# The last norm's factors multiplied in behind the product with W, and sent there over DRAM

## The chip, the cores and the metric

The kernel runs on one core of one Trainium2 chip. The metric is the device time of one launch in microseconds (us); lower is better. Unless a single run is named, times are medians of the fast runs of a kernel, with the lowest and highest in brackets. The engines are TensorE (PE; PEld is its weight load), VectorE (DVE), ScalarE (ACT), GpSimd (POOL) and SyncE (SP), which issues nearly all transfers of this kernel, in order.

## The reference, cut to what matters

The input is 4 images of 128 channels and 64 x 64 points, so 16,384 tokens of 128 values. Layer 0 is a convolution with window attention. Layer 1 is a linear attention and a feed-forward part, each behind a normalisation of every token. The change touches the last normalisation and the product with W that follows it.

```python
def _ln_t(v, eps=1e-5):                      # each token on its own
    m = jnp.mean(v, axis=-1, keepdims=True)
    s = jnp.var(v, axis=-1, keepdims=True)
    return (v - m) / jnp.sqrt(s + eps)

def _L1_ffn_ref(x, W, V, gamma, beta):
    Wx = jnp.einsum('bti,hi->bth', x, W)
    # mean and variance of Wx over all tokens, then normalised by them
    # ... then y_t = sigmoid(wx_t + y_{t-1} V^T), a scan over the tokens
...
t = _to_tokens(layer0(x))
t = t + _L1_attn_ref(_ln_t(t), ...)
t = t + _L1_ffn_ref(_ln_t(t), ...)           # the last norm and W
```

The statistics over all tokens mean that nothing of the final part can start before the last token's product with W is there. Hence the kernel has a long middle, band after band, and a tail.

## The kernel before

The tokens are worked off in 16 bands of 1024 (two halves of 512 in layer 1, four windows in layer 0). PE alternates between the window attention of one band and layer 1 of the band before. A half's tokens stand on the partitions (128 tokens by 4 groups); its last norm writes `xn`, four transposes on PE turn it, ACT copies it out of the bank, and the product with W follows. Besides that, the residual stream `h.x` is turned as well (`keep`), since it is needed at the end.

```python
ENGINES = [... for e in ("PE", "DVE", "Activation", "Pool")]    # held to the source's order; SP is not
...
    def keep(h):
        rs = p1.tile([P, SEG, HSEGS], F32, tag="rs_o", name="rs_o")
        nc.scalar.copy(rs, turned(h.x, 0, 4).rearrange("p (k s) -> p s k", s=SEG))
        nc.sync.dma_start(resd[h.b][:, h.hb], rs.rearrange("p s k -> p (s k)"))

    def turn_last(h):                        # four transposes and a copy
        h.xl = p2.tile([P, 512], F32, tag="xl2", name="xl2")
        nc.scalar.copy(h.xl, turned(h.xn, 0, 4))

    def product(h):
        wps = bank()
        nc.tensor.matmul(wps, fwT, h.xl, start=True, stop=True)
        nc.scalar.copy(wx[:, h.b, h.hb], wps.rearrange("p (k s) -> p s k", s=SEG))
        nc.vector.bn_stats(stats[:, h.b * NH + h.hb, :], ...)
```

The window attention has a small round trip of its own: the softmax's denominators are packed into `dc`, inverted, written to DRAM (`rd`) and read back spread over the partitions (`rden`); GpSimd multiplies the heads' output by it (`oT`), and the output projection on PE needs `oT`.

```python
        nc.sync.dma_start(dc, den[::HD, :])
        ...
        nc.vector.reciprocal(rc, dc)
        rd = dram4.tile([HEADS, BR * WT], F32, tag="rd", name="rd")
        nc.sync.dma_start(rd.rearrange("h (a e) -> (h a) e", e=16), rc)
        rden = p1.tile([P, BR * WT], F32, tag="rden", name="rden")
        nc.sync.dma_start(rden, rd.unsqueeze(1).to_broadcast([HEADS, HD, BR * WT]))
```

## Time and profile before

| | before |
|---|---|
| time | 935.57 us (933.84 to 939.02), 3 runs |
| mean granted clock of PE | 0.975 |
| PE, DVE, ACT, POOL busy | 94%, 80%, 58%, 28% |
| one band in the middle | 50.3 us |
| transfers | 53,045 packets, 63.46 MB |

PE is the bound: from 100 to 800 us it has work in 99 to 100% of the time at full clock, and the other engines have slack. The lines for this stand in the prediction.

```profile
DVE dc L423 <- DMA dc<-den: 7.5, 4, 3.4
```

A line number below, such as L221, is the line in the kernel that is being shown; the change and the experiments move lines by a few.

### The profile page before, as it was taken

The numbers are of one execution on the slowest core, as the hardware profiler recorded it, in microseconds if no ns is written. First come the engines' busy times: TensorE is split into PE (matmuls) and PEld (weight loads), VectorE is DVE, ScalarE is ACT, GpSimd is POOL, SyncE is SP. The second block draws the span as 40 slices with busy tenths as digits, with TensorE's granted clock in tenths as the row PEclk, the third lists the DMA queues.
The fourth block names the chain that finished last, engine by engine and source line by source line (L and its number), as shares of the span: only waits on it lengthen the run. The fifth ranks groups of instructions, "written<-read, shape, count | busy, mean of one in ns | idle before, by whom it ended". The sixth has DMA issues, their size and how long they took to land.

```text
span 930.9 us, 26534 instructions
## 1 busy us (share of the span) xinstructions
PE 876.9 (94%) x10508; PEld 656.1 (70%) x10508; DVE 741.1 (80%) x2452; ACT 539.1 (58%) x1010; POOL 262.4 (28%) x359
## 2 busy tenths in 40 slices
PE   4978999999999999999999999999999999987985
PEld 3756777877777777777787777787777777755442
DVE  6464978888897988797988888798878786676886
ACT  3755566565756565656656575656566665422552
POOL 2122131413232322313041323232232312121184
PEclk9988999999999999999999999999999999988897
DMA  4111121121222121212121121212121111102853
GB/s 121 34 44 56 47 72 37 54 57 57 59 63 59 49 57 50 69 49 73 37 56 57 52 59 60 62 48 62 48 66 48 49 37 60 43 24 73 345 205 129
DMA packets 53045, 63.46 MB, mean 68 GB/s; under 512 B 22960, under 2 KB 33840, under 8 KB 52400
## 3 DMA queue, kind: packets, MB, share of 16 engines
q1 hardware_dynamic: 51184, 56.91, 19.8%
q10 hardware_dynamic: 1728, 4.77, 1.3%
q8 instruction: 85, 1.39, 0.6%
q14 instruction: 48, 0.39, 0.1%
HBM read 35.44 MB, written 17.30 MB: 57 GB/s over the span
## 4 chain that ended last, share of the span: by engine, by line
PE 60%; DVE 26%; issue 4%; ACT 4%; DMA 3%; POOL 3%; ACTq 0%; SPq 0%; DVEq 0%; POOLq 0%
DVE y L288 8%; PE bank L337 8%; PE bank L465 6%; PE bank L382 6%; PE bank L212 6%; PE bank L494 5%; PE bank L400 4%; PE bank L350 4%; PE bank L412 4%; PE bank L602 3%; DVE st L191 2%; PE bank L815 2%; PE bank L537 2%; PE bank L573 2%; DVE state L562 2%
## 5 line engine op out<-in xcount | busy, mean ns | idle before, releaser
L288 DVE SCALAR_TENSOR_TENSOR y<-ypad,cpe_w,y 128x512 f32<-128x512 f32 x240 | 189.8, 791 | 15.1 <-ACT y L286 11.7
L391 ACT ACTIVATE es<-bank 128x512 f32<-128x512 f32 x256 | 132.2, 603 | 77.1 <-PE bank L382 77.1
L440 POOL TENSOR_TENSOR oT<-o_sb,rden 128x512 f32<-128x512 f32 x64 | 86.6, 1354 | 243.1 <-DMA rden<-rd 165.8
L195 POOL TENSOR_SCALAR rs<-mv 128x4 f32<-128x4 f32 (+2 forms) x100 | 25.1, 251 | 364.4 <-DVE mv L193 163.2
L203 DVE TENSOR_SCALAR xn<-x,mv,rs 128x128 f32<-128x128 f32 x256 | 90.8, 416 | 26.5 <-POOL rs L196 26.5
L196 POOL TENSOR_TENSOR rs<-rs,mhalf 128x4 f32<-128x4 f32 (+2 forms) x100 | 106.2, 1062 | 8.3
L382 PEld LDWEIGHTS bank<-q,k 32*128 32x128 f32 x3072 | 97.7, 189 | 7.8 <-ACT k L345 6.6
L382 PE MATMUL bank<-q,k 32*128 32x96 f32 (+1 forms) x3072 | 96.3, 270 | 1.1 <-ACT k L345 1.1
L412 PEld LDWEIGHTS bank<-es,v_sb 128*32 128x32 f32 x3072 | 56.8, 110 | 30.2 <-issue 18.6
L465 PE MATMUL bank<-woT,oT 128*128 128x128 f32 x512 | 68.1, 289 | 5.7 <-POOL oT L440 5.7
L465 PEld LDWEIGHTS bank<-woT,oT 128*128 128x128 f32 x512 | 64.8, 202 | 9.7 <-POOL oT L440 7.3
L412 PE MATMUL bank<-es,v_sb 128*32 128x96 f32 (+1 forms) x3072 | 70.1, 240 | 0.0
L494 PE MATMUL bank<-xl,awT 128*128 128x512 f32 x128 | 70.0, 630 | 0.0
L400 PE MATMUL bank<-es,ones 128*32 128x512 f32 x512 | 69.1, 612 | 0.0
L357 ACT COPY v_sb<-bank 128x512 f32<-128x512 f32 x64 | 37.5, 586 | 53.5 <-PE bank L350 42.2
L337 PE MATMUL bank<-y2w,wqT 128*128 128x256 f32 x256 | 66.4, 382 | 1.0 <-DVE y2w L288 1.0
L337 PE MATMUL bank<-y2w,wkT 128*128 128x256 f32 x256 | 65.8, 380 | 0.0
L350 PE MATMUL bank<-wvT,y2w 128*128 128x256 f32 x256 | 65.8, 380 | 0.0
L345 ACT COPY q<-bank 128x512 f32<-128x512 f32 x64 | 37.6, 587 | 41.3 <-PE bank L337 39.2
L345 ACT COPY k<-bank 128x512 f32<-128x512 f32 x64 | 37.3, 583 | 36.8 <-PE bank L337 36.7
L191 DVE BATCH_NORM_STATS2 st<-x 128x6 f32<-128x128 f32 x256 | 55.5, 280 | 1.1
L337 PEld LDWEIGHTS bank<-y2w,wqT 128*128 128x128 f32 x256 | 45.8, 194 | 12.8 <-issue 7.2
(124 smaller groups left out, 1728.4 us busy)
## 6 DMA issues: line engine op xcount, KB each, us to landing
rden<-rd SPq DMA_DIRECT2D x64, 256.0 KB
v_sb<-v_sb SPq DMA_DIRECT2D x128, 64.0 KB
resd<-rs_o SPq DMA_DIRECT2D x32, 256.0 KB
out<-ot SPq DMA_DIRECT2D x32, 256.0 KB
xin<-in_xt SPq DMA_DIRECT2D x15, 512.0 KB
res<-resd SPq DMA_DIRECT2D x2, 2048.0 KB
res<-resd ACTq DMA_DIRECT2D x2, 2048.0 KB
dc<-den SPq DMA_DIRECT2D x64, 8.0 KB
```

Source lines behind the costliest of these rows:

```text
L196: nc.gpsimd.tensor_tensor(rs[:, :n], rs[:, :n], mhalf[:, :n], ALU.pow)
L203: nc.vector.tensor_scalar(xn[:, j, :], piece, mv[:, j, 0:1], rs[:, j : j + 1], ALU.subtract, ALU.mult)
L288: nc.vector.scalar_tensor_tensor(y2, src, cpe_w[:, tap : tap + 1], y2, ALU.mult, ALU.add)
L337: nc.tensor.matmul(pps[:, br * WT : (br + 1) * WT], wT[:, br * P : (br + 1) * P], y2, start=True, stop=True,)
L350: nc.tensor.matmul(vps[:, e * 256 : (e + 1) * 256], y2[:, e * P : (e + 1) * P], wvT, start=True, stop=True,)
L382: nc.tensor.matmul(sps[h][:, cols], w["k"][rows, k0 : k0 + P], w["q"][rows, cols], start=False, stop=(br, n) == pieces[-1],)
L391: nc.scalar.activation(es, sps[h], AF.Exp, scale=scale)
L400: nc.tensor.matmul(dps[rows], ones[:, :HD], w["es", h], start=True, stop=True)
L412: nc.tensor.matmul(ops[rows, cols], w["v"][:, n, c0 : c0 + HD], w["es", h][:, cols], start=(br, n) == pieces[0], stop=(br, n) == pieces[-1],)
L440: nc.gpsimd.tensor_tensor(oTs[n][:, :, :, wj * WS : (wj + 1) * WS], w["o"].rearrange("p (a r c) -> p a r c", a=BR, c=WS), w["rden"].rearra ...
L465: nc.tensor.matmul(yps[:, j * P : (j + 1) * P], oT[:, br, t], woT[:, br, :], start=br == 0, stop=br == BR - 1,)
L494: nc.tensor.matmul(zps, awT[:, m * P : (m + 1) * P], h.xl, start=True, stop=True)
```

## The change

The intent is to take work off PE. A norm is (x - m) r with a mean m and a factor r for each token. If W is centred once (each row minus its mean), then W (x - m) r = (Wc x) r: the product can be applied to the turned residual stream, which `keep` makes anyway, and the factor r multiplied in behind it. The transposes of `xn` and two ACT copies fall away. But behind the product the tokens stand on the free axis, so their factors are needed as a row, the same on all 128 partitions. They go there over DRAM: a small transfer `send` writes 512 factors, and a broadcast `spread` reads them back into `rs_b`. Both are issued ahead of time, and SP is held to the source's order too. The load of the band after next is issued one window later. Two buffer counts change as well and are not in the cut below: `xn` has two buffers instead of three, `rs_o` two instead of one.

```diff
-ENGINES = [getattr(mybir.EngineType, e) for e in ("PE", "DVE", "Activation", "Pool")]
+ENGINES = [getattr(mybir.EngineType, e) for e in ("PE", "DVE", "Activation", "Pool", "SP")]
...
+    def send(h):
+        h.there = dram4.tile([SEG, 4, P // SEG], F32, tag="rs_d", name="rs_d")
+        nc.sync.dma_start(h.there.rearrange("s j n -> n s j"), h.found[2])
+
+    def spread(h):
+        h.rs = p2.tile([P, 512], F32, tag="rs_b", name="rs_b")
+        nc.sync.dma_start(h.rs, h.there.rearrange("s j n -> (s j n)").partition_broadcast(P))
...
-    def turn_last(h):
-        h.xl = p2.tile([P, 512], F32, tag="xl2", name="xl2")
-        nc.scalar.copy(h.xl, turned(h.xn, 0, 4))
...
-        nc.tensor.matmul(wps, fwT, h.xl, start=True, stop=True)
-        nc.scalar.copy(wx[:, h.b, h.hb], wps.rearrange("p (k s) -> p s k", s=SEG))
+        nc.tensor.matmul(wps, fwT, h.xs.rearrange("p s k -> p (s k)"), start=True, stop=True)
+        w = wx[:, h.b, h.hb].rearrange("p s k -> p (s k)")
+        nc.vector.tensor_tensor(w, wps, h.rs, ALU.mult)
...
-            (norm, z), (product, y), None,
+            (send, z), None,
             (output0, a), (measure, a), None,
-            (turn_last, z), None,
+            (product, y), (spread, z), None,
... (the second half of the order and the end likewise)
-        if i < len(places) and wj == 1 and n + 2 < len(bands):
+        if i < len(places) and wj == 2 and n + 2 < len(bands):
             load(n + 2)
```

With `SEG` = 32 the tensor in DRAM is 32 x 4 x 4 values, and each of the 512 factors is a run of 4 bytes of its own. The order is that in which the product's columns stand, so that the multiply reads its factors straight.

More of the change, by code (lines that the diff above doesn't have):

```diff
@@ L80, in conv_attn_hybrid @@
     )
+    center = const.tile([P, P], F32, name="center")
+    nc.vector.tensor_scalar(center, ident, -1.0 / P, None, ALU.add)
     mhalf = const.tile([P, NCH], F32, name="mhalf")
@@ L139, in prepare, with centre @@
         nc.vector.tensor_scalar(ab1, ab[:, :2], 1.0, None, ALU.add)
+    def centre(w):
+        cps = bank()[:, : w.shape[1]]
+        nc.tensor.matmul(cps, center, w, start=True, stop=True)
+        nc.vector.tensor_copy(w, cps)
     dmax = const.tile([P, 16], F32, name="dmax")
@@ L484, in norm @@
     def norm(h):
-        h.xn = normed(h.found, p3, "xn")
+        h.xn = normed(h.found, p2, "xn")
     def turn(h):
@@ L587, in attend @@
             nc.vector.scalar_tensor_tensor(x, nv[:, i, :P], rd[:, i, :], x, ALU.mult, ALU.add)
-    def keep(h):
-        rs = p1.tile([P, SEG, HSEGS], F32, tag="rs_o", name="rs_o")
-        nc.scalar.copy(rs, turned(h.x, 0, 4).rearrange("p (k s) -> p s k", s=SEG))
-        nc.sync.dma_start(resd[h.b][:, h.hb], rs.rearrange("p s k -> p (s k)"))
-    def turn_last(h):
-        h.xl = p2.tile([P, 512], F32, tag="xl2", name="xl2")
-        nc.scalar.copy(h.xl, turned(h.xn, 0, 4))
+    def send(h):
[4 more added lines that the diff above has]
+        nc.sync.dma_start(h.rs, h.there.rearrange("s j n -> (s j n)").partition_broadcast(P))
+    def keep(h):
+        h.xs = p2.tile([P, SEG, HSEGS], F32, tag="rs_o", name="rs_o")
+        nc.scalar.copy(h.xs, turned(h.x, 0, 4).rearrange("p (k s) -> p s k", s=SEG))
+        nc.sync.dma_start(resd[h.b][:, h.hb], h.xs.rearrange("p s k -> p (s k)"))
     def product(h):
         wps = bank()
-        nc.tensor.matmul(wps, fwT, h.xl, start=True, stop=True)
-        nc.scalar.copy(wx[:, h.b, h.hb], wps.rearrange("p (k s) -> p s k", s=SEG))
-        nc.vector.bn_stats(
-            stats[:, h.b * NH + h.hb, :], wx[:, h.b, h.hb].rearrange("p s k -> p (s k)")
-        )
+        nc.tensor.matmul(wps, fwT, h.xs.rearrange("p s k -> p (s k)"), start=True, stop=True)
+        w = wx[:, h.b, h.hb].rearrange("p s k -> p (s k)")
+        nc.vector.tensor_tensor(w, wps, h.rs, ALU.mult)
+        nc.vector.bn_stats(stats[:, h.b * NH + h.hb, :], w)
     def layer1(n, last):
@@ L633, in layer1 @@
             (scores, c), (keep, a), None,
-            (accumulate, c), (norm, a), None,
+            (accumulate, c), (send, a), None,
             (attend, c, 0), None,
-            (turn_last, a), (attend, c, 1), (measure, c), None,
+            (attend, c, 1), (measure, c), (spread, a), None,
         ]
@@ L647, in layer1_end @@
     def layer1_end(y, z):
-        norm(z)
+        send(z)
+        keep(z)
+        yield
         product(y)
-        yield
-        keep(z)
-        turn_last(z)
+        spread(z)
         yield
@@ L709, in conv_attn_hybrid @@
                 behind = layer1(m, halves.pop(m - 1, (None, None)))
+        if i == 2:
+            centre(fwT)
         between(i, 0)
```

## The prediction

> **What bounds the kernel now.** I read the page's busy table first, then the busy time by stretches, then the groups of instructions, and last the timeline of one band of 1024 tokens (the middle of the run repeats every 50.3 us, one band each, 16 bands).
>
> ```profile
> PE 876.9 (94%) x10508; PEld 656.1 (70%) x10508; DVE 741.1 (80%) x2452; ACT 539.1 (58%) x1010; POOL 262.4 (28%) x359
> ...
> 300.00:400.00 100.00, 99.14 (x1282) 76.11 (x1278) 84.66 (x287) 61.57 (x113) 28.98 (x41) 1.00 0.20 56
> 700.00:800.00 100.00, 99.79 (x1320) 76.81 (x1314) 77.56 (x257) 60.70 (x112) 23.48 (x31) 1.00 0.16 48
> 800.00:850.00 50.00, 43.96 (x358) 33.65 (x358) 37.33 (x141) 15.25 (x27) 9.79 (x13) 0.93 0.09 30
> ```
>
> From 100 to 800 us TensorE (PE) is never without work and its clock is 1.00. The second engine, VectorE (DVE), has 15% slack, ScalarE (ACT) 38%. Before 100 and after 800 us the program is bound by latency instead. So in the middle only PE time counts, and at the two ends only the length of chains.
>
> Busy PE time overstates a matmul, because they overlap. I therefore take each group's cost as the distance from its start to the next group's start. Four groups of transposes of the normalised tokens (xn) run in each band:
>
> ```profile
> 471.39 1.01 PE L212 MATMUL bank<-ident,xn 128*128 128x128 f32 x4
> 472.23 0.39 PE L573 MATMUL bank<-v,aT 128*128 128x129 f32 x2
> ...
> 482.15 0.60 PE L212 MATMUL bank<-ident,xn 128*128 128x128 f32 x4
> 482.58 1.03 PE L337 MATMUL bank<-y2w,wkT 128*128 128x256 f32 x4
> ```
>
> These two are the ones that the change removes (first half and second half of a band). The first costs 0.84 us, because it is fed by DVE writing its four pieces just then (1.11 us); the second, whose pieces are long ready, costs 0.43 us. The groups' table would have suggested far more, 4 x 288 ns = 1.15 us each.
>
> ```profile
> L203 DVE TENSOR_SCALAR xn<-x,mv,rs 128x128 f32<-128x128 f32 x256 | 90.8, 416 | 26.5 <-POOL rs L196 26.5
> L212 PE MATMUL bank<-ident,xn 128*128 128x128 f32 x256 | 46.1, 288 | 5.1 <-DVE xn L203 4.8
> L604 DVE BATCH_NORM_STATS2 stats<-wx 128x6 f32<-128x512 f32 x32 | 22.1, 689 | 29.6 <-ACT wx L603 29.5
> L472 DVE TENSOR_TENSOR x<-bank,xin 128x512 f32<-128x512 f32 x32 | 21.9, 685 | 33.7 <-PE bank L465 33.7
> L603 ACT COPY wx<-bank 128x512 f32<-128x512 f32 x32 | 20.1, 629 | 3.9 <-PE bank L602 3.9
> L597 ACT COPY xl<-bank 128x512 f32<-128x512 f32 x32 | 18.8, 588 | 20.7 <-PE bank L212 20.7
> ```
>
> **What the Trainium skill says.** "Perfetto Trace Analysis", section Identifying the Most-Contended Engine, says that matmul occupancy is no good measure for TensorE, as pipelined instructions distort it. The trace agrees: 0.43 us from start to start against 0.60 us of busy time. "DMA: Bandwidth & Descriptors", section Why a DMA increments its semaphore by 16 and not by 1, says that a transfer uses the largest number of engines up to 16 that divides the slowest dimension of both sides. The trace agrees for the existing broadcast rden, whose outer dimension is the 4 heads: its packets fill a share of 0.24 to 0.26, four engines of 16, and it lands 5.3 us after its issue:
>
> ```profile
> 42.27 0.59 SPq L431 DMA_DIRECT2D rden<-rd  x1
> 47.54 1.27 POOL L440 TENSOR_TENSOR oT<-o_sb,rden 128x512 f32<-128x512 f32 x1 [13.54 <-DMA rden<-rd]
> ```
>
> The same page, section Rules for kernel authors, says that a non-contiguous last dimension becomes one descriptor per element; no run here shows that yet, but the new small transfer is of that kind. "TensorE: Matmul & The Clock Gate", section Part 1: The HAM clock gate, says that idleness halves the clock. The trace agrees: after PE idled 4.4 us at 59 us, one round of logits took 2.89 us instead of 1.48. So stalls at the ends cost about double.
>
> **The change, part by part.**
>
> Removed from PE: 32 groups of four transposes. Per band 0.84 + 0.43 = 1.27 us. The product itself stays, and one 128x128 matmul that centres W is added once.
>
> Removed from DVE: the normalisation of 32 halves. In the timeline the two of a band last 1.11 and 2.06 us (the second runs beside a GpSimd multiply). Added: a multiply of a bank by the spread factors, 128x512; by the same shape of L472, 0.69 us each. Net per band 3.17 - 1.38 = 1.8 us less. Removed from ACT: two copies per half, 588 + 629 ns, 2.4 us per band. Neither engine bounds, so this is worth nothing directly.
>
> Added on the queue: per half a send of 512 single values (4 bytes each) and a broadcast of 256 KB. The send's outer dimension is 4, so I expect four engines with 128 descriptors each. The 128 descriptors of dc took 1.1 engine-us altogether (shares 0.12 and 0.22 of 16 engines over 0.2 us each), 9 ns each; at 9 to 12 ns the send needs 1.1 to 1.5 us on its engines. With the 1.5 us that rd needs from issue until rden can follow (804.74 to 806.27), the send should take 2.5 to 3 us (estimate). The broadcast has 128 rows outermost, so 16 engines: 8 packets of 2 KB each at some 110 ns (rden's 32 packets per engine in 3.5 us), about 0.9 us plus latency, 2.5 to 3 us when nothing is ahead of it (estimate).
>
> Moved: the first half's product goes two slots later, behind the output projection L465. So PE reaches L465 sooner, by 1.06 us (the product) and 0.84 us (the transposes). But L465 needs oT, which follows rden: issued at 471.12, oT started at 477.26, ended at 478.53, and PE used it at 479.39. Slack 0.86 us. In the new order I count 5.1 us of PE work from the start of that window's logits to L465, and oT ready at about 5.5 us. So PE will stall there for some 0.4 to 0.5 us, and the saving is 1.27 - 0.45 = 0.8 us per band. Over some 15 bands: -12 us.
>
> The second half's factors are the tight ones on DVE. Its broadcast is issued right behind rden, waits on the four shared engines, and lands some 17.5 us into the window; DVE would want it at 15.7. That is a stall of 1.8 us, but DVE stood there for 1.8 us before too (stats waiting for wx, 29.5 us over 18 waits). I take it as neutral: the transposes that follow find their pieces just in time.
>
> Ends. Start: the load of the third band, which was issued at 11.7 us, now stands in the queue in front of dc at about 44 us, so the early stall grows: +1 us. Between 800 and 850 us two groups of transposes leave a chain that PE latency sets: -2 us. At the very end the last half had normalise, turn, copy, product, copy, statistics: rs at 852.38, statistics at 857.31. Now send, broadcast, multiply: 2.7 + 2.8 + 0.7 = 6.2 us against 4.9, and the reload of the residual stream waits for the multiply as well: +2 us.
>
> Sum: -12 + 1 - 2 + 2 = -11, that is 935.6 - 11 = about 924 us.
>
> **The rivals.**
>
> First, everything hides: no stall at L465, and DVE's freed time removes the rest of PE's small waits (2.5 us on x at L212, some 4 us at L575). Then 1.27 + 0.4 us per band, 25 us in all, ends still +1: about 911. For it speaks that the change was evidently arranged around the waits; against it the 0.86 us slack of oT.
>
> Second, the factors' round trip over DRAM takes the removed work's place: if the 4-byte writes are much slower than I estimate, or the broadcast queues behind rden and the loads, DVE stands 3 us longer per band, the convolution's taps come late, and PE waits for turned tokens by 1 to 2 us. Then the gain is eaten: 935 to 945. For it speaks that DVE and the queue both work strictly in order; against it DVE's 15% slack, and that the change takes another 1.8 us per band from it.
>
> Third, the naive sum: 128 transposes at 288 ns, 37 us, giving 899. The start-to-start distances speak against it.
>
> Fourth, the order of the transfers alone does something: in the middle no PE wait is put down to a DMA, so I expect nothing there.
>
> **Range and chances.** The size per band is the uncertainty: 0.2 to 1.6 us times 15 is -3 to -24, with the ends -2 to +5. So 911 to 936. Faster by over 2% means under 916.9, a gain of 18.7 us, which needs nearly all of the 1.27 us: 0.15. Slower by over 2% would need a new stall of 2.5 us per band beyond the saving: 0.02.
>
> **What would show it.** The distance between bands should fall from 50.3 to about 49.5 us; PE should wait for oT at L465 in most bands; the new multiply on DVE should wait 1 to 2 us for its broadcast in the second halves and not in the first; packets should rise by 32 x 512 + 32 x 128 = 20,480, less a little; the send should take about 2.7 us. Last product to last statistics should be longer by about 2 us. The prediction is wrong if bands fall by 1.5 us or more (then L465 doesn't wait), or if PE waits for DVE after the multiply.

## More of the kernel before

One more view is of use for what follows, the chain of work that ended last, followed back from the last instruction; the shares are of the span:

```profile
PE 60%; DVE 26%; issue 4%; ACT 4%; DMA 3%; POOL 3%; ACTq 0%; SPq 0%; DVEq 0%; POOLq 0%
```

Only 3% of the chain is a transfer. Two waits for the small round trip, of SP's queue and of DVE over the whole span, serve for comparison later (us in total, times, longest):

```profile
SPq L431 <- DMA rd<-rc: 51.4, 45, 2.1
```

## The result, and the profile after

The changed kernel takes 1148.60 us (1145.22 to 1151.02, 4 runs) against 935.64 us (933.84 to 939.02) of the kernel before in the same rounds. The ratio is 1.2268, with a 95% interval of 1.2216 to 1.2320: slower by 23%. A ratio here is always the mean time of one kernel's fast runs over the mean of the other's of the same rounds, so it is not quite the ratio of the medians quoted.

The prediction of 924 us was wrong, in direction and by far more than its range. First the page of the changed kernel: its busy time, then the chain that ended last, by engine and by line.

```profile
PE 926.3 (81%) x10382; PEld 684.2 (60%) x10382; DVE 712.0 (62%) x2358; ACT 510.3 (44%) x946; POOL 257.9 (22%) x359
...
DMA 39%; DVE 27%; PE 23%; issue 4%; POOL 3%; ACT 3%; SPq 1%; ACTq 0%; DVEq 0%; POOLq 0%
DMA rd<-rc 10%; DVE y L297 7%; DMA rs_b<-rs_d 7%; DMA dc<-den 7%; DMA rden<-rd 6%; DMA rs_d<-rs 5%; DVE st L200 3%; PE bank L346 3%; PE bank L474 3%; PE bank L503 2%; PE bank L391 2%; DMA res<-resd 2%; PE bank L221 2%; PE bank L359 2%; PE b
```

The engines did what they were meant to: PE has 126 matmuls fewer (10,508 to 10,382), DVE is busy for 29.1 us less. But transfers now hold 39% of the chain instead of 3%. The striking point is which: the new ones (`rs_d` and `rs_b`) hold 12%, and the old round trip of the softmax denominators (`dc`, `rd`, `rden`) 23%. The busy time by stretches says the same of the middle. Its columns are busy us and instructions of PE, PEld, DVE, ACT and POOL, then the granted clock, the share of the DMA engines, and GB/s:

```profile
300.00:400.00 100.00, 77.69 (x955) 60.60 (x951) 58.22 (x220) 42.83 (x78) 22.67 (x34) 0.91 0.24 50
```

No engine is busy for more than 78% of the time here, and the DMA engines' share is 0.24. So this is a chain of waits. PE's and DVE's waits between 100 and 1000 us, and the waits of SP's queue over the whole span, name the links (us in total, times, longest):

```profile
PE bank L221 <- DVE xn L212: 117.7, 25, 10.5
PE bank L474 <- POOL oT L449: 15.7, 13, 3.7
```

```profile
DVE wx L619 <- DMA rs_b<-rs_d: 105.9, 13, 9.7
DVE dc L432 <- DMA dc<-den: 97.0, 16, 11.6
```

```profile
SPq L440 <- DMA rd<-rc: 154.7, 64, 8.2
...
SPq L606 <- DMA rs_d<-rs: 132.9, 18, 12.1
```

PE waits for DVE's norm; DVE waits for the factors and for `dc`; SP waits up to 12.1 us until a `send` has landed and it may issue the broadcast, and up to 8.2 us for `rd` (2.1 before).

The timeline of one band shows the mechanism; it is a band with two of the longest waits (PE's 25 waits for `xn` last 4.7 us in the mean). First SP's queue (start, length of the issue), without the `v_sb` loads:

```profile
506.30 0.55 SPq L601 DMA_DIRECT2D rs_d<-rs  x1
...
518.27 0.32 SPq L606 DMA_DIRECT2D rs_b<-rs_d  x1
...
519.15 1.89 SPq L414 DMA_DIRECT2D dc<-den  x1
521.09 0.57 SPq L601 DMA_DIRECT2D rs_d<-rs  x1
528.12 0.32 SPq L438 DMA_DIRECT2D rd<-rc  x1
532.19 0.54 SPq L440 DMA_DIRECT2D rden<-rd  x1
```

From the issue of the first `send` until the broadcast may follow are 12.0 us. Everything behind it in the source's order is held up with it: `dc` is issued only at 519.15, although ACT had its source `den` ready at 511.8. The broadcast and the store of the residual stream, 256 KB each, go out just before `dc`, the second `send` right behind it. What DVE and PE do meanwhile (the brackets give the idle time before and what ended it):

```profile
527.62 0.17 DVE L432 TENSOR_TENSOR dc<-dc,pad_c 128x16 f32<-128x16 f32 x1 [11.22 <-DMA dc<-den]
```

```profile
529.92 1.15 PE L221 MATMUL bank<-ident,xn 128*128 128x128 f32 x4 [10.19 <-DVE xn L212]
```

DVE works in order, stands for 11.22 us at `dc`, and so comes late to the norm that PE needs: PE stands for 10.19 us. Then its clock is down, at 0.50, and the round of logits at 531.40 takes 2.72 us where it took 1.48. Of the 11.22 us 2.75 lie before the issue of `dc`, the rest between its issue and its landing; over the whole run it is 33 of 108 us. `rd`, issued at 528.12, takes 4.1 us until `rden` may follow. SP's timeline shows in each of 14 bands one `rd` that is issued while a `send` is on its way: these take 3.5 to 8.6 us, 7.2 in the median, the other 50 of the run 1.5. So the small transfers are not only issued late; those on the way together with a `send` land late too. A stretch of 2 us in this wait, with the same columns as above, shows how idle the transfers themselves are:

```profile
524.00:526.00 2.00, 0.00 (x0) 0.00 (x0) 0.00 (x0) 0.00 (x0) 0.00 (x0) 0.50 0.01 0
```

From 524.0 to 527.6 hardly anything moves: no engine works, 0 GB/s, a DMA share of 0.01 to 0.09. The core waits for writes that the records hardly count as work.

At the end, the queue is quiet, and a `send` is seen with nothing big beside it (the store issued in front of it has moved its last packet at 1048.6):

```profile
1048.36 0.53 SPq L601 DMA_DIRECT2D rs_d<-rs  x1
1057.70 0.31 SPq L606 DMA_DIRECT2D rs_b<-rs_d  x1
```

It takes 9.3 us for 2 KB, and 11.8 the second time (1058.07 to 1069.82), with the store of the residual stream beside it. The prediction had 2.5 to 3. The DMA records tell where in these 9.3 us the time is. In two stretches of it:

```profile
1049.50:1050.40 0.90, 0.64 (x4) 0.28 (x2) 0.83 (x6) 0.00 (x0) 0.00 (x0) 1.00 0.31 2
1054.00:1057.70 3.70, 0.00 (x0) 0.00 (x0) 0.00 (x0) 0.00 (x0) 0.00 (x0) 1.00 0.00 0
```

All 512 packets, of 9 ns each, are recorded in the 0.9 us from 1049.52 to 1050.40. From there until the broadcast may follow, 7.3 us, the DMA share is 0.00. So what is long is not the packets' recorded time but the time from the last packet to the landing.

Where the time came from, along the run: I cut each profiled run at the start of the first output projection of the second band and of the fourteenth. Before: 126.3 us to the first cut, 604.0 for the 12 bands between (50.3 each), 200.6 to the end. After: 126.1, 764.4 (63.7 each), 258.8. So the middle lost 160.4 us, the end 58.2, the start nothing.

### The profile page after: what moved, and what is told of

It reads as the page before. It is cut to its first block, busy times and chain, and to the rows that moved or that the text cites.

```text
span 1149.3 us, 26192 instructions
## 1 busy us (share of the span) xinstructions
PE 926.3 (81%) x10382; PEld 684.2 (60%) x10382; DVE 712.0 (62%) x2358; ACT 510.3 (44%) x946; POOL 257.9 (22%) x359
## 4 chain that ended last, share of the span: by engine, by line
DMA 39%; DVE 27%; PE 23%; issue 4%; POOL 3%; ACT 3%; SPq 1%; ACTq 0%; DVEq 0%; POOLq 0%
DMA rd<-rc 10%; DVE y L297 7%; DMA rs_b<-rs_d 7%; DMA dc<-den 7%; DMA rden<-rd 6%; DMA rs_d<-rs 5%; DVE st L200 3%; PE bank L346 3%; PE bank L474 3%; PE bank L503 2%; PE bank L391 2%; DMA res<-resd 2%; PE bank L221 2%; PE bank L359 2%; PE bank L520 2%
## 5 line engine op out<-in xcount | busy, mean ns | idle before, releaser
L297 DVE SCALAR_TENSOR_TENSOR y<-ypad,cpe_w,y 128x512 f32<-128x512 f32 x240 | 184.9, 771 | 14.3 <-ACT y L295 10.8
L221 PE MATMUL bank<-ident,xn 128*128 128x128 f32 x128 | 34.2, 404 | 130.5 <-DVE xn L212 129.7
L391 PEld LDWEIGHTS bank<-q,k 32*128 32x128 f32 x3072 | 111.7, 212 | 3.9 <-ACT k L354 1.8
L619 DVE TENSOR_TENSOR wx<-bank,rs_b 128x512 f32<-128x512 f32 x32 | 22.0, 689 | 147.3 <-DMA rs_b<-rs_d 140.0
L391 PE MATMUL bank<-q,k 32*128 32x96 f32 (+1 forms) x3072 | 110.2, 295 | 1.1 <-ACT k L354 1.1
L221 PEld LDWEIGHTS bank<-ident,xn 128*128 128x128 f32 x128 | 21.4, 169 | 147.5 <-issue 134.1
L498 ACT COPY xl<-bank 128x512 f32<-128x512 f32 x32 | 18.8, 587 | 156.8 <-PE bank L221 156.8
L432 DVE TENSOR_TENSOR dc<-dc,pad_c 128x16 f32<-128x16 f32 x64 | 13.9, 217 | 108.3 <-DMA dc<-den 108.3
L346 PE MATMUL bank<-y2w,wkT 128*128 128x256 f32 x256 | 75.7, 424 | 0.0
L481 DVE TENSOR_TENSOR x<-bank,xin 128x512 f32<-128x512 f32 x32 | 22.0, 688 | 82.7 <-PE bank L474 82.7
```

What stands on the lines that cost most here:

```text
L221: nc.tensor.transpose(tps[:, j * P : (j + 1) * P], xn[:, j0 + j, :], ident)
L297: nc.vector.scalar_tensor_tensor(y2, src, cpe_w[:, tap : tap + 1], y2, ALU.mult, ALU.add)
L346: nc.tensor.matmul(pps[:, br * WT : (br + 1) * WT], wT[:, br * P : (br + 1) * P], y2, start=True, stop=True,)
L391: nc.tensor.matmul(sps[h][:, cols], w["k"][rows, k0 : k0 + P], w["q"][rows, cols], start=False, stop=(br, n) == pieces[-1],)
```

## The experiments

My theory after the result: the 512 writes of 4 bytes are slow in themselves, because many of them go to the same short stretch of DRAM, and what hurts is mostly what queues behind them. The rivals: the order to which SP is now held (R1); the four engines that the transfer's outer dimension allows (R2); the number of descriptors or the 4 bytes as such (R3); and that only the direct wait for the factors counts (R4). A last question is where the 12 us went that the middle was to gain. Unless said otherwise, each kernel is the changed one with the edit shown, and gave a correct result. The "send" durations are from the issue of the `send` to the issue of its broadcast, for the last half but one, where the queue is quiet.

**Rows of 16 bytes** (row16). The four factors of a partition stay together in DRAM: 128 runs of 16 bytes, partitions outermost. In exchange the multiply reads its factors in steps of 512 bytes.

```diff
-        h.there = dram4.tile([SEG, 4, P // SEG], F32, tag="rs_d", name="rs_d")
-        nc.sync.dma_start(h.there.rearrange("s j n -> n s j"), h.found[2])
+        h.there = dram4.tile([P, 4], F32, tag="rs_d", name="rs_d")
+        nc.sync.dma_start(h.there, h.found[2])
...
-        nc.vector.tensor_tensor(w, wps, h.rs, ALU.mult)
+        rs = h.rs.rearrange("p (n s j) -> p s j n", n=P // SEG, j=4)
+        nc.vector.tensor_tensor(w.rearrange("p (s j n) -> p s j n", ...), wps..., rs, ALU.mult)
```

> The factors are sent as 128 rows of 16 bytes (partition outermost) instead of 512 single values, and the multiply reads them in a permuted order; all else as in the changed kernel. Theory A (the many 4-byte descriptors make the send take 12 us, and the queue and VectorE stand behind it): the send takes 1.5 to 2.5 us from issue to the broadcast's issue, and the time falls from 1149 to 915-930 us. Theory B (holding the queue to the source's order is what costs): the time stays above 1080 us. Theory C (the 256 KB broadcast loads the engines that rden and dc need): stays above 1080 us too, with the send short.

Measured: 931.43 us (929.62 to 933.72), ratio to the kernel before 0.9978 (0.9942 to 1.0014). The send at the end:

```profile
843.47 0.32 SPq L601 DMA_DIRECT2D rs_d<-rs  x1
844.92 0.32 SPq L606 DMA_DIRECT2D rs_b<-rs_d  x1
```

1.45 us instead of 9.3 for the same 2 KB, and all of the loss is gone with it; the `rd` that are issued beside a `send` take 1.5 us again instead of 7.2. The shape of the write is the cause. The price of the permuted read is seen in the groups of instructions of the changed kernel and of this one (busy us, mean ns, idle before):

```profile
L619 DVE TENSOR_TENSOR wx<-bank,rs_b 128x512 f32<-128x512 f32 x32 | 22.0, 689 | 147.3 <-DMA rs_b<-rs_d 140.0 <-PE bank L503 7.3
```

```profile
L620 DVE TENSOR_TENSOR wx<-bank,rs_b 128x512 f32<-128x512 f32 x32 | 33.6, 1051 | 29.8 <-DMA rs_b<-rs_d 25.2 <-PE bank L409 2.4 <-PE bank L503 2.2
```

0.36 us more for each multiply, on an engine with slack; the wait for the factors fell from 140.0 to 25.2 us. PE's longest wait in the middle of this run (100 to 800 us) is the one that the prediction was about (0.6 us before):

```profile
PE bank L474 <- POOL oT L449: 9.4, 12, 1.3
```

**Single values on 16 engines** (val4x16). Still 512 runs of 4 bytes in 2 KB, but with the partitions as the outer dimension, for R2.

```diff
+        h.there = dram4.tile([4, P], F32, tag="rs_d", name="rs_d")
+        nc.sync.dma_start(h.there.rearrange("j p -> p j"), h.found[2])
```

> Still 512 single values of 4 bytes, but with the 128 partitions as the outermost dimension of both sides, so that 16 engines can share them (32 descriptors each instead of 128); the multiply permutes on reading. Theory A1 (the cost is per descriptor and engine, some 90 ns each in a row on four engines): send 3.5 to 5 us, time 925-970 us. Theory A2 (small writes into the same lines of DRAM follow one another whoever issues them): send stays at 9 to 12 us and the time above 1080 us.

Measured: 1094.61 us (1094.41 to 1096.14), ratio 1.1723 (1.1687 to 1.1758). The send:

```profile
993.17 0.37 SPq L601 DMA_DIRECT2D rs_d<-rs  x1
1001.34 0.32 SPq L606 DMA_DIRECT2D rs_b<-rs_d  x1
```

8.2 us: four times the engines save 1.1 of 9.3 us. In the total the ratio falls from 1.2268 to 1.1723, about a quarter of the loss, though the multiply's read is permuted here too (1036 ns instead of 689). So R2 has a part, but three quarters of the loss stay.

**No transfers** (no_transfer). `send` and `spread` are taken out, and the multiply reads ones. The result is wrong (it stays within the tolerance, as the factors are near one and a normalisation follows).

```diff
-        nc.sync.dma_start(h.there.rearrange("s j n -> n s j"), h.found[2])
-        nc.sync.dma_start(h.rs, h.there.rearrange("s j n -> (s j n)").partition_broadcast(P))
-        nc.vector.tensor_tensor(w, wps, h.rs, ALU.mult)
+        nc.vector.tensor_tensor(w, wps, fives, ALU.mult)     # fives: a constant tile of ones
```

> Wrong result on purpose: no send and no broadcast, the multiply reads a constant tile. It shows what the change in the work of the engines is worth by itself. My prediction's sum without transfer stalls: bands 49.0 to 49.5 us apart, 905-922 us. If it stays above 1000 us, the transfers are not the cause at all (Theory D: the moved product or the multiply on VectorE).

Measured: 916.67 us (915.13 to 921.94), ratio 0.9812 (0.9778 to 0.9846). The whole loss belongs to the two new transfers; without them the rest of the change is a gain of 1.9%.

**SP's order left free** (free_sp), for R1. SP is taken out of the engines that are held to the source's order; the order of the instructions on the other four engines is the same as in the changed kernel.

```diff
-... for e in ("PE", "DVE", "Activation", "Pool", "SP")]
+... for e in ("PE", "DVE", "Activation", "Pool")]
```

> The changed kernel with the queue's order left to the scheduler as before; the other four engines' order is the same, instruction by instruction. Theory A: still slow, above 1050 us, as the 12 us send stays. Theory B: back to about 915-940 us.

Measured: 1205.66 us (1204.35 to 1207.51), ratio 1.2916 (1.2875 to 1.2958). It is worse than with the order held: SP now waits 256.5 us instead of 132.9 for the sends. R1 falls, and the order that the change brings along is worth 5% with this send.

**Factors sent but not used** (not_used), for R4. The transfers stay, the multiply reads ones (wrong, within the tolerance).

> Wrong factors on purpose: the changed kernel with its 512-value send and its broadcast, but the multiply reads ones, so no engine waits for the factors. It splits the 1149 us into the direct wait of VectorE and the transfers that stand behind the send in the queue. If the direct wait is the cause: 920-950 us. If the queue behind it (dc, rd, rden late) is: above 1050 us.

Measured: 1062.13 us (1060.70 to 1065.49), ratio 1.1370 (1.1326 to 1.1414). The waits of DVE and of SP's queue over the span:

```profile
DVE dc L432 <- DMA dc<-den: 94.8, 22, 9.3
```

```profile
SPq L440 <- DMA rd<-rc: 140.3, 64, 7.4
```

So of the 23% some 14 stay when no multiply waits for the factors. R4 explains the smaller part; the larger is `dc`, `rd` and `rden`, which come late behind the sends. (One direct wait is left in this run: behind the last product DVE stands for 18.6 us until the last broadcast has landed, DVE mv L775. So the 14 hold a little that isn't the middle's queue; per band 8.6 of the 13.4 us stay.)

**Single values, each in its own 512 bytes** (val4_lines; one look). As not_used, with 16 engines, 512 runs of 4 bytes, but 512 bytes apart in DRAM. The broadcast is cut to a small read, and the multiply reads ones, so it is to be compared with no_transfer and not_used.

```diff
+        h.there = dram4.tile([P, 4, P], F32, tag="rs_d", name="rs_d")
+        nc.sync.dma_start(h.there[:, :, 0], h.found[2])
+        nc.sync.dma_start(h.rs[:16, 0:1], h.there.rearrange("p j w -> (p j) w")[:16, 0:1])
```

> Wrong factors on purpose: 512 values of 4 bytes on 16 engines as in val4x16, each into its own 512-byte line of DRAM, with a small read behind it. In the quiet queue at the end the send took 8.2 us in val4x16, where 512 values share four such lines. If the writes hinder one another because they share lines: 2 to 3.5 us. If each small write costs on its own: 7 to 9 us.

Measured: 923.78 us (1 run). The send:

```profile
837.13 0.53 SPq L601 DMA_DIRECT2D rs_d<-rs  x1
839.30 0.32 SPq L606 DMA_DIRECT2D rs_b<-rs_d  x1
```

2.2 us, with the same number of descriptors, bytes and engines as the 8.2 us of val4x16. In both runs the records show the packets over within 0.4 us; from the last one to the broadcast it is 0.6 us here and 6.9 there. R3 falls: neither the 4 bytes nor the 512 descriptors are slow. They are slow when they stand side by side.

**The same, 64 bytes apart** (val4_64; one look): `h.there = dram4.tile([P, 4, 16], ...)`.

> As the run with every 4-byte value in its own line of 512 bytes (send 2.2 us at the end, 923.78 us in all), but with a distance of 64 bytes between values, so eight values share 512 bytes and none shares 64. Theory A: writes to the same few bytes come one after the other, at some 16 to 18 ns for each of the 512 when all stand in 2 KB, and eight in a line no longer show: send of 2 to 3 us, 920 to 928 us. Theory B: the unit in which they hinder each other is larger than 512 bytes (the 512 values stand in 32 KB here, 256 KB there): send of 5 to 9 us, 1000 us and more. Factors are not used, so the result is wrong on purpose by the small difference from one.

Measured: 924.14 us (1 run), send 2.5 us. Eight values share 512 bytes here and it hardly shows.

**128 values only, side by side** (val4_few; one look). Of the four columns of factors one is sent, into one run of 512 bytes. The broadcast is cut to a small read and the multiply reads ones, as in val4_lines.

```diff
+        h.there = dram4.tile([1, P], F32, tag="rs_d", name="rs_d")
+        nc.sync.dma_start(h.there.rearrange("j p -> p j"), h.found[2][:, :1])
```

> As the runs with single values whose factors aren't used, but only 128 of the 512 values are sent, 4 bytes each, packed into one run of 512 bytes, on 16 engines. As many values share a 512-byte line (128) and a 64-byte stretch (16) as in the 8.2 us send of 512 values. Theory A: the hindrance is a count for all writes to the tensor, one after the other at 16 ns: 128 of them take about 2 to 2.5 us, 920 to 930 us in all. Theory B: the hindrance is in each line, and lines go side by side: the send still takes 7 to 9 us, 1030 to 1070 us in all. The result is wrong on purpose by the small difference of the factors from one.

Measured: 965.64 us (1 run). The send:

```profile
871.04 0.32 SPq L601 DMA_DIRECT2D rs_d<-rs  x1
878.15 0.32 SPq L606 DMA_DIRECT2D rs_b<-rs_d  x1
```

7.1 us for a quarter of the values: theory B is right for the send. As far as these two points go (128 values in 512 bytes 7.1 us, 512 in 2 KB 8.2), its duration follows how many writes share a stretch, not how many there are. The total, however, is far below what theory B named (1030 to 1070), so this expectation was half a miss. The `rd` beside a `send` are nearly as late as in not_used (6.0 us in the median against 6.6), but DVE waits only 19.8 us for `dc` between 100 and 800 us, against 74.8 there. The run differs from not_used in two ways: the fewer writes, and the 256 KB broadcast in front of `dc`, which is missing. Which of them spares `dc`, these runs do not show. They also leave open how long the stretch is: 8 values in 512 bytes are harmless (val4_64), 128 are not, and 32 rows of 16 bytes are harmless as well (row16).

**Rows of 16 bytes on four engines** (row16x4; one look): `h.there = dram4.tile([4, P // 4 + 4, 4], ...)`, written as `h.there[:, : P // 4, :]`.

> Rows of 16 bytes as in the run of 931.43 us, but in an order whose outer dimension is 4, so that four engines write 32 rows each. Theory A: 32 descriptors of some 10 to 20 ns add at most 0.5 us: send at the end of 1.5 to 2.2 us, 928 to 938 us in all. Theory B: the engine count is what made small sends slow: send of 3 us or more, above 945 us.

Measured: 946.22 us (1 run), send 2.0 us. The duration is as theory A had it; the total is 8 us above its range, and nearer to theory B's. DVE's wait for the factors between 100 and 800 us is 31.2 us against 19.8 in row16. The edit changes the broadcast too: it reads four runs of 512 bytes for each partition instead of one of 2 KB (74,165 packets in all against 62,261). So whether the engine count or the smaller packets cost these 12 us is not separated; the send's 8 us are not a matter of the engine count.

**Which part of the remaining gain is lost where.** row16 was 931.43 us, no_transfer 916.67. The suspect was `rden`, which fills only four engines, so that `oT` is late and the broadcast queues behind it. Two edits were tried together and alone.

```diff
# rden4: four transfers, one for each head, whose outer dimension is 32
-        nc.sync.dma_start(rden, rd.unsqueeze(1).to_broadcast([HEADS, HD, BR * WT]))
+        for h in range(HEADS):
+            nc.sync.dma_start(rden[h * HD : (h + 1) * HD], rd[h].partition_broadcast(HD))
```

```diff
# early: the first half's product before the output projection again, its multiply behind
-            (send, z), None,
-            (output0, a), (measure, a), None,
-            (product, y), (spread, z), None,
+            (send, z), (product, y), None,
+            (output0, a), (measure, a), None,
+            (factored, y), (spread, z), None,
```

Both, on row16 (row16_both):

> On top of the 16-byte rows: (1) the broadcast rden goes out as four transfers, one per head, whose slowest dimension is 32, so that 16 engines carry each instead of four for all; (2) the first half's product runs on TensorE in front of the output projection again, and only its multiply stays behind it. If the wait for oT at the output projection is what takes the rest of the gain (row16 931, without transfers 917), PE's wait there vanishes, bands come 48.7 to 49.3 us apart, and the time is 908-920 us. If the rest is lost in the multiply on VectorE (1.04 us, waiting for its factors), it stays at 925-932 us.

Measured: 916.63 us (915.88 to 920.10), ratio 0.9799 (0.9766 to 0.9833). PE's wait for `oT` in the middle is gone, and PE is busy for 99.80 of the 100 us from 300 to 400.

The early product alone (row16_early):

> Only (2) of these: the product in front of the output projection. PE has 1.05 us of work to fill the wait for oT of 1 to 1.5 us per band, but rden comes no sooner: 915-927 us. If moving the product was not what opened the wait: unchanged, 929-933 us.

Measured: 939.01 us (937.49 to 942.86), ratio 1.0044 (1.0000 to 1.0089), slower than row16. PE's wait for `oT` is gone here too, and yet a band takes 50.9 us against 50.1. PE's longest waits between 100 and 800 us are now 8.7 us in 13 waits for `x` and 1.9 us in 5 for `v`. They moved from `oT` to what DVE makes. Measured from the start of each group on PE to the start of the next, the transposes of `xn` cost 1.52 us a band against 1.01 in row16, those of `x` 1.99 against 1.78, and the logits 5.93 against 5.70. PE arrives earlier, at work that DVE has not finished. A stall that is taken away at one place came back, larger, at others.

`rden` in four parts alone, on row16 (row16_rden4):

> Rows of 16 bytes for the send, and the broadcast of rden split by head into four transfers whose outer dimension is 32, so that each fills 16 engines; the product stays behind the output projection. It separates the two parts of the run that had both (916.63 us). Theory A: rden on four engines was the wait (oT late at the output projection, dc behind rden at the start), and the early product is then needless: 914 to 920 us, PE without a wait for oT from 100 to 800 us. Theory B: the two parts only gain together, since a shorter rden alone only moves PE's wait from oT to the next thing in the window: 922 to 930 us. If it stays at 930 or above, the gain of the earlier run came from the early product once oT is in time.

Measured: 913.90 us (912.79 to 917.74), ratio 0.9823 (0.9805 to 0.9842). Theory A: the split is the fix, the early product is needless. PE still waits for `oT`, 3.9 us in 5 bands, which theory A had not expected.

`rden` in four parts on the kernel before, without the change (before_rden4):

> The kernel before, with the broadcast of rden split by head into four transfers that fill 16 engines, and nothing else. Theory A (mine): in the middle PE waits for oT there only 0.6 us in all, so the split is worth nothing per band and only shortens the stall of the first bands by 3 to 5 us: 925 to 929 us. Then the gain of the change with the split (913.9 us) beyond that is the removed transposes' own, some 1 us a band. Theory B: the split alone is the gain: 912 to 918 us, and the change itself is worth nothing.

Measured: 928.04 us (926.18 to 929.77), ratio 0.9950 (0.9928 to 0.9973): theory A. The split alone is worth 0.5%, at the start (123.2 us to the first cut instead of 126.3), and nothing per band (50.3 us as before). The rest of the gain needs the change and the split together: row16, the change without the split, had 0.9978.

**The order of the transfers on the kernel before** (before_sp).

```diff
-... for e in ("PE", "DVE", "Activation", "Pool")]
+... for e in ("PE", "DVE", "Activation", "Pool", "SP")]
-        if i < len(places) and wj == 1 and n + 2 < len(bands):
+        if i < len(places) and wj == 2 and n + 2 < len(bands):
```

> The kernel before, with nothing of the new product: only the fifth engine held to the source's order and the load of the band after next issued one window step later. Theory A (mine): it is neutral, 930 to 938 us, since in the middle PE waits for no transfer. Theory B: the order alone costs or gains: beyond 945 it would explain part of the loss, below 925 it would be the real source of what the repaired kernels gain.

Measured: 930.56 us (927.91 to 931.33), ratio 0.9997 (0.9975 to 1.0019). Neutral: this part of the change neither costs nor gains by itself.

**The last half by the old path.** The very last half has nothing to hide a round trip behind, so it gets its norm, transposes and product as before. First with both edits (best):

> The run with both (16-byte rows, rden in four parts, early product), and for the very last half the old path: normalise, turn, product, copy, statistics, with no send and no broadcast. The chain at the end was 2.4 us longer than in the kernel before from the last factors to the reload of the residual stream. Theory A: this chain sets the end, so 2 to 3 us come back: 913 to 915 us, faster than the kernel before by 2.0 to 2.3%. Theory B: the end hangs on something beside it (the statistics of the last band's other half), and it stays at 916 to 917.

Measured: 914.70 us (913.78 to 916.68), ratio 0.9837 (0.9819 to 0.9856). Its profiled run is shorter behind the second cut (199.1 us against 202.8 in row16_both), but by the ratio there is no gain over row16_both. Then with the split alone (row16_rden4_end):

```diff
     def layer1_end(y, z):
-        send(z)
+        norm(z)
         keep(z)
         yield
         product(y)
-        spread(z)
         yield
-        product(z)
+        # four transposes of z.xn, copy, matmul with the centred W, copy, statistics
```

> The best form so far (16-byte rows, rden split, product behind the output projection, 913.9 us), with the very last half by the old path (normalise, turn, product, copy, statistics, no send). From the start of the fifteenth band to the end that form took 202.5 us against 200.6 in the kernel before and 199.1 in the form with the early product and the old path. Theory A: 2 to 3 us come back: 910 to 912 us. Theory B: it is within the scatter: 913 to 915 us.

Measured: 909.97 us (907.33 to 912.19) against 932.84 us (929.34 to 935.24), ratio 0.9749 (0.9726 to 0.9772). This beats both kernels: the one before by 2.5% in the same rounds, the changed one by 21% (medians of different rounds). PE is at 94% again, as before the change, with 22 us less to do (854.8 us busy). From 100 to 800 us it waits 3.9 us for `oT` and 2.6 us for `x`. The profiled runs in one table, cut as described above:

| kernel | to the 2nd band | per band (12 bands) | from the 14th band to the end |
|---|---|---|---|
| before | 126.3 | 50.33 | 200.6 |
| after | 126.1 | 63.70 | 258.8 |
| not_used | 125.8 | 58.89 | 226.5 |
| no_transfer | 126.4 | 49.78 | 196.5 |
| row16 | 126.4 | 50.07 | 202.3 |
| row16_early | 125.4 | 50.93 | 202.1 |
| row16_both | 123.3 | 49.35 | 202.8 |
| row16_rden4 | 121.9 | 49.30 | 202.5 |
| before_rden4 | 123.2 | 50.30 | 198.7 |
| row16_rden4_end | 122.3 | 49.21 | 197.7 |

(The expectation of the last run speaks of the fifteenth band's start where this table says fourteenth; it is the same cut.) The end of a run scatters: three kernels whose end is that of before (before, before_sp with 198.4, before_rden4) lie between 198.4 and 200.6. So of the 4.8 us between row16_rden4 and row16_rden4_end I count on the predicted 2 to 3.

## Why the prediction was wrong

**The step that failed** is the size of the send: "the send should take 2.5 to 3 us (estimate)". It took 9.3 us in the quiet queue and 12.0 in the band shown. Of the sum's two terms the first was right: 9 to 12 ns for a descriptor, taken from `dc`, made 1.1 to 1.5 us, and the records show 9 ns each, 0.9 us in all. The number of descriptors was right as well (packets rose by 21,121, predicted 20,480 or a little less). The second term was wrong: 1.5 us for all the rest, taken from `rd`, which writes 128 rows of 64 bytes. For 512 values of 4 bytes that stand side by side in 2 KB of DRAM the rest was 8.4 us, of which 7.3 lie behind the last packet. The number is not what costs: the same 512 take 2.2 us when they stand apart (val4_lines) and 8.2 us packed (val4x16). The case I knew and the case I applied it to differed in just what mattered.

**The second rival** had the mechanism: "if the 4-byte writes are much slower than I estimate". Its size, 935 to 945, was wrong as it counted DVE's direct wait alone. The measured chain has a link that I did not work out: SP issues in order, and a send that lands late holds up the window attention's round trip, in the middle once in every band `dc` behind the first send and `rd` behind the second. not_used shows that this is the larger part, 14 of the 23%. From 100 to 1000 us, about 14 bands of 63.7 us, PE waits 117.7 + 15.7 us for `xn` and `oT`, 9.5 us a band. Besides, PE's busy time grew by 49.4 us although its work shrank, 3.1 us for each of 16 bands, at a mean clock of 0.892 instead of 0.975. The two make most of the 13.4 us that a band lost. The chance of 0.02 for slower by over 2% rested on "a new stall of 2.5 us per band" being out of reach; with a send four times as long it was not.

**What was right**, as the repaired kernels show. The removed transposes were to save 1.27 us a band: from start to start of PE's groups, all transposes of `xn` cost 2.23 us a band before and 1.01 in row16, so 1.22. (The product, put at 1.06 us, costs 1.01 by the same measure, which changes no sum.) The stall at the output projection behind `rden` came where it was expected, but larger: predicted 0.4 to 0.5 us a band. In row16 PE waits 9.4 us for `oT` in the 14 bands between 100 and 800 us, 0.7 us a band, and the groups in front of the projection grew by 0.74; in no_transfer by 0.89. The second halves' factors were to make DVE wait 1.8 us: row16 shows 19.8 us over 11 waits, 1.8 each. DVE's saving of 1.8 us a band is 29.1 / 16 = 1.8. The tail from the last factors to the reload of the residual stream was to be 2 us longer: 4.4 us before (852.38 to 856.74) and 6.8 in row16 (848.26 to 855.07), 2.4 longer; in the changed kernel itself it is 21.9 (1053.13 to 1075.02), 4.9 of them until the send could be issued. The fourth rival, that the order alone does nothing, held (before_sp).

**What the sum would have been.** With a send of 1.45 us, row16 gains 0.26 us a band where 0.8 was predicted, because of the larger stall for `oT` and a second one on `x` (6.3 us in all), which the slower permuted multiply on DVE may add to; that last part was not tested. With `rden` on 16 engines the gain is 1.03 us a band. So the intent was sound, and the prediction of 924 lies between the two forms (931.43 and 913.90) that have a send of the size I assumed. The prediction saw that `rden` used four engines, and did not ask what the change would be worth if it did not. Not shown to be right is the 1 us at the start: the first cut is at 126.3 before and 126.1 after.

## What to carry to other kernels

When a new transfer is sized from an old one, compare where the bytes land, and not only the number and size of descriptors; if no transfer of the trace writes short runs side by side into DRAM, the estimate has no basis, and the range must say so. The time from the last packet to the landing is a term of its own: here the 9 ns for each packet held, and the 1.5 us for the rest did not. Lay out a small round trip so that a partition's values stay together in DRAM, and pay for the order on the reading engine if that has slack (0.36 us here against some 8). And when a transfer enters a queue that works in order, look at who stands behind it: its neighbours lost more than its own reader.

## What the Trainium skill lacked or had wrong

- "DMA: Bandwidth & Descriptors", section Specifications, says that below 512 bytes a transfer is done by read-modify-write; section Rules for kernel authors that a non-contiguous last dimension becomes one descriptor per element. The second agrees (21,121 packets more). Whether the first is at work no run here shows. Neither tells this: 512 runs of 4 bytes take 2.2 us at 512 bytes apart and 2.5 us at 64 bytes apart, but 8.2 us packed in 2 KB on the same 16 engines, and 128 of them packed in 512 bytes still 7.1 us. A figure for short writes that share a stretch of DRAM is missing.
- The same page has no figure for what such a transfer does to those behind it in the same queue: the longest wait for `rd` rose from 2.1 to 8.2 us, and those issued beside a send took 7.2 us in the median instead of 1.5, while the DMA engines' recorded share in a wait was 0.01 to 0.09.
- The same page's rule for the number of engines (section Why a DMA increments its semaphore by 16 and not by 1) held: while `rden` moves at the start, the share is 0.24 to 0.26 before and 0.69 with the split (row16_rden4, 45.5 to 46.0 us). The runs add what it is worth: 0.5% for `rden` in the kernel before, and 931.43 to 913.90 us with the repaired change, in different rounds (ratios to before of 0.9978 and 0.9823).
- "SBUF — State Buffer", section Door 1: The DMA port swizzle (why `[64,N]` ≈ `[32,N]`), says that accesses which leave a line of 16 bytes at each step pay a penalty, without a figure for DVE. Here a multiply of 128 x 512 whose one operand is read in steps of 512 bytes took 1051 ns instead of 689, and in steps of 128 bytes 1036 (val4x16). That the lines are the reason no run here shows.
